# A two-layer graph network on one core: look-ups and gathers moved around the branch, and the last batch stored in natural order

## The chip, the cores and the metric

The kernel runs on one core of a Trainium2 chip. The metric is the device time of one execution in microseconds (us); a single core runs, so it is also the slowest. Five engines work side by side, each through its own queue of instructions and in its order: PE (TensorE, matmuls), DVE (VectorE), ACT (ScalarE), POOL (GpSimd) and SP (SyncE). Plain DMAs are issued by SP and ACT, and those with a list of row numbers (gathers and scatters) by POOL. An engine waits for another engine or for a DMA through semaphores.

## The reference

x is 32 batches of 512 rows of 512 floats, adj one 512 x 512 matrix, mostly zero, with weights between 0.05 and 1 on the diagonal and on some other entries. Two layers, each with a layer norm and a ReLU ahead of it:

```python
h = jnp.maximum(_layernorm(x, axis=-1), 0.0)
x = x + (jnp.einsum('nm,bmd->bnd', adj, h) @ weight + bias)       # layer 0
h = jnp.maximum(_layernorm(x, axis=-1), 0.0)
q, k, v = h @ Wq + bq, h @ Wk + bk, h @ Wv + bv                   # 8 heads
scores = q k^T / sqrt(64) + (1.0 - adj) * -1000000000.0
x = x + softmax(scores) v @ Wo + bo                               # layer 1
```

The mask is so strong that a row's softmax comes down to the column with the greatest adj, where that is certain. Layer 1 is then, for each row, one row of h (its source, `idx`) times the product Wv Wo, plus a constant row `cvo`.

## The kernel before, in words

A prologue (not touched) multiplies Wv and Wo, finds `idx`, and tests on the device whether each row has one clear source and few enough rows are sources. `single_path` is the path for that case.

**The loop.** `run_phase` goes through loops b = 0 to 32. Loop b holds, in this order on PE, layer 0 of batch b (seven products in the manner of Strassen, `product`, L534, whose results DVE adds onto x at L590), the aggregation adj @ h of batch b+1, and layer 1 of batch b-1 (seven products, results taken by DVE at L580 and ACT at L582). A batch's x lies in one of five tiles (`xs`).

**The order.** Each loop has 21 steps, one for each product or other piece of PE work. `put(batch, step, f)` hangs a piece of work of the other engines on a step, and the engines' queues get the work in that order, which no scheduler changes. POOL's indirect DMAs are also held back in time: `behind` makes each wait for the last result that an engine took from PE's accumulators before it in this order (`tick`), so that it goes out "in step".

**The plan.** Most entries of adj are zero. `Plan` (L1027) finds, in loops 0 to 3 and beside the dense work, an order of the rows in which adj becomes mostly empty. `xi` is the list of x rows in the new order for every batch, `gi` that of some extra rows. `schedule` hangs the plan's work on (loop, step) pairs. What the change touches: `tables` gathers the four row tiles of the reordered adj (`ap<-atd`, L1292), `tables_g` the three of the extra rows (`ag`), and `look_1` looks up, for each of the four tiles of `idx`, the new position of a row (`pi<-posd`, L1292), a gather of 128 numbers, after `posd` is written in loop 2. In loop 6 DVE casts `pi` at L1307 (`whole_pi`), PE turns the result over at L1297, and from this the second look-up `pq` (`look_2`) and the lists `place` and `home` are made.

**The branch.** Loops 0 to 3 run dense and in natural order. Ahead of loop FIRST = 4 every engine loads a flag and branches (L980 to L982). If the plan fits, loops 4 to 32 run with the sparse aggregation `spread` (L651, L654, L657): it multiplies h by the tiles of `ap`, one row tile after the other, and the normalised extra rows (`plan.HG`, in the tile `adjT`) by `ag`. From then on x of a batch is gathered in the new order by POOL (`load_x`, L506; in the profile under its helper's line, L497), the extra rows too (`load_g`, L666, `at<-in_x_dram,gi`), and the finished batches are scattered back to natural rows of the output by POOL (`store_rows`, L518). The extra rows of batches 5 and 6 are normalised by `lead` (statistics on ACT at L396, offset on DVE at L407, the ReLU on ACT at L381); later ones together with x.

**Layer 1 and its DRAM tables.** The h rows that are sources are written to a compact DRAM table `hs` (`put_h`; from a natural-order batch a POOL scatter for each of the four tiles, L694) and read back in another arrangement into `hc` (`get_h`, four SP DMAs, L705, each waiting for all four scatters), which DVE transposes to `hT` (L756). The products' result z is transposed by DVE (L770) and written to DRAM (`put_z`, L775), and POOL's gather `x<-z` adds each row's z to x (`finish`).

**The end.** For batches 29 and 30 (`back`), x is turned back to natural order: POOL scatters it into a DRAM tile (`turn_back`, L470), SP reads it back (`come_back`, L480), and the stores to the output are plain ones by SP or ACT (L512). Batch 31 stays in the new order. Its layer 1 is `layer1_rows`: POOL gathers, for all rows, the source rows of h (`get_all`, by `plan.pq`), PE transposes them (L717, copied by ACT at L718) and multiplies them row tile by row tile (r = 0 to 3, L729), DVE adds the result (L732), and the tile is scattered to the output by POOL (L518). After r = 0 DVE adds z of batch 29, and POOL starts to fetch z of batch 30 (`fetch`); after r = 2 and r = 3 DVE adds it, three tiles and one (L789).

Lines that the text names belong to the kernel before.

## Time and profile before

| What | Value |
|---|---|
| times of three runs | 1012.4, 1013.54, 1016.65 us; median 1013.54 |
| the profiled execution's own time | 1015.4 us |
| its span, from the first to the last instruction | 1013.7 us |
| mean granted clock of PE | 0.995 |
| busy: PE, DVE, POOL, ACT | 988.4, 801.1, 590.0, 585.3 us |
| moved by DMA | 208.89 MB, 206 GB/s over the span |
| branch passed by PE | 177.54 us |
| loops 4, 5, 6, 7, 8 | 28.93, 31.93, 31.54, 28.82, 28.82 us |
| PE begins the row tiles of the last batch | 985.63 us |
| last landing of a store | 1008.79 us |

All times count from the start of the span. The page gives sums over the whole span; queries of the trace give the same for a stretch, the waits of one engine with what ended them, and each engine's timeline. In a timeline a row is: start, length, engine, line, operation, output<-input, how many of them in a row, and in brackets the idle time ahead with what ended it ("issue" is time in which nothing that the profile shows was waited for). Issue and landing times of DMAs come from the trace's records of them.

### The profile page before, as it was taken

What the parts mean: (1) busy time and instruction counts of PE and PEld (TensorE: products, weight loads), DVE (VectorE), ACT (ScalarE), POOL (GpSimd) and SP (SyncE); (2) the same over time, 40 slices, a digit from 0 to 9 for tenths busy, and PEclk for the clock granted to TensorE, in tenths of its full rate; (3) what the DMA queues carried; (4) which work ended last, traced back from release to release, by engine and by line L of the source; (5) the groups of instructions that cost most, each with busy time, mean ns of one, the idle gap of its engine ahead of it and who ended that gap; (6) DMA issues with size and microseconds to landing.
All of it is one profiled execution on the core that took longest, in us unless ns stands there. A gap on an engine that the chain in (4) does not pass through costs nothing.

```text
span 1013.7 us, 17267 instructions
## 1 busy us (share of the span) xinstructions
PE 988.4 (98%) x5627; PEld 886.6 (87%) x5627; DVE 801.1 (79%) x1792; ACT 585.3 (58%) x1282; POOL 590.0 (58%) x667
## 2 busy tenths in 40 slices
PE   9999998999999999999999999999999999999985
PEld 7478887988899999999999999999999999999882
DVE  6998887767888777778887777778887777788773
ACT  4756444556665555566755555667655556676230
POOL 1033267656666666666666666666666666666543
PEclk9999999999999999999999999999999999999998
DMA  9214578889898888888888888888878888888867
GB/s 337 100 56 141 101 221 235 207 206 233 194 231 203 199 214 209 221 228 221 208 202 202 208 215 213 229 220 215 206 195 207 220 206 230 221 216 210 214 201 248
DMA packets 161883, 208.89 MB, mean 206 GB/s; under 512 B 16556, under 2 KB 104376, under 8 KB 161784
## 3 DMA queue, kind: packets, MB, share of 16 engines
q0 software_dynamic: 44544, 120.10, 48.4%
q1 hardware_dynamic: 115480, 85.66, 29.5%
q10 hardware_dynamic: 1760, 1.93, 0.6%
q8 instruction: 46, 0.75, 0.3%
q14 instruction: 53, 0.43, 0.2%
HBM read 123.55 MB, written 84.09 MB: 205 GB/s over the span
## 4 chain that ended last, share of the span: by engine, by line
PE 84%; DVE 7%; issue 3%; DMA 3%; ACT 1%; POOL 1%; SPq 0%; POOLq 0%; DVEq 0%; ACTq 0%
PE mm L534 59%; PE mm L654 13%; PE mm L657 7%; PE mm L651 2%; PE mm L675 1%; DVE st L363 1%; DMA hc<-hs 1%; DMA ap<-in_adj_dram,xi 1%; PE mm L273 1%; DVE x L590 1%; DVE x L629 0%; DMA hs<-h,dest 0%; PE pt L171 0%; DMA x<-xn 0%; ACT h L381 0%
## 5 line engine op out<-in xcount | busy, mean ns | idle before, releaser
L590 DVE TENSOR_TENSOR x<-mm,x 128x512 f32<-128x512 f32 x217 | 148.4, 686 | 135.9 <-PE mm L534 100.4
L497 POOL DMA_INDIRECT x<-z,pplace x96 | 153.4, 1598 | 81.5 <-ACT yT L662 40.9
L381 ACT ACTIVATE h<-x,off,rstd 128x512 f32<-128x512 f32 x256 | 196.1, 804 | 6.9 <-DVE off L372 3.6
L534 PE MATMUL mm<-w_t,sel 128*128 128x256 f32 x744 | 171.9, 380 | 3.1 <-DVE x L590 2.8
L367 ACT ACTIVATE rstd<-mv,eps 128x2 f32<-128x2 f32 (+1 forms) x90 | 26.3, 292 | 241.1 <-DVE mv L364 226.0
L534 PEld LDWEIGHTS mm<-w_t,sel 128*128 128x128 f32 x744 | 140.5, 190 | 23.6 <-DVE x L590 4.2
L363 DVE BATCH_NORM_STATS2 st<-x 128x6 f32<-128x512 f32 x234 | 157.5, 673 | 1.1
L654 PE MATMUL mm<-ap,h 128*128 128x256 f32 x648 | 157.8, 380 | 0.0
L518 POOL DMA_INDIRECT out_dram<-x,xi x100 | 124.6, 1246 | 45.7 <-DVE zs L580 19.8
L497 POOL DMA_INDIRECT x<-in_x_dram,xi x108 | 103.8, 961 | 72.0 <-issue 29.5
L654 PEld LDWEIGHTS mm<-ap,h 128*128 128x128 f32 x648 | 114.9, 191 | 11.1
L497 POOL DMA_INDIRECT at<-in_x_dram,gi x81 | 77.2, 953 | 72.0 <-DVE st L363 22.3
L534 PE MATMUL mm<-w_s,yT 128*128 128x256 f32 x496 | 117.3, 379 | 0.8 <-PE mm L534 0.8
L534 PE MATMUL mm<-hTs,wvo_t 128*128 128x168 f32 x720 | 113.6, 307 | 2.1 <-ACT zs L582 2.1
L534 PEld LDWEIGHTS mm<-hTs,wvo_t 128*128 128x128 f32 x720 | 105.4, 190 | 3.1 <-ACT zs L582 3.1
L582 ACT ACTIVATE zs<-mm,cvo_c 128x168 f32<-128x168 f32 x240 | 82.8, 397 | 41.4 <-PE mm L534 29.0
L534 PEld LDWEIGHTS mm<-w_s,yT 128*128 128x128 f32 x496 | 92.8, 190 | 12.3 <-issue 1.0
L657 PEld LDWEIGHTS mm<-ag,adjT 128*128 128x128 f32 x648 | 89.3, 191 | 5.6
L657 PE MATMUL mm<-ag,adjT 128*128 128x128 f32 x648 | 89.7, 275 | 0.0
L629 DVE TENSOR_TENSOR x<-x,b_r 128x512 f32<-128x512 f32 x124 | 83.9, 678 | 0.0
L662 ACT COPY yT<-mm 128x512 f32<-128x512 f32 x108 | 61.5, 570 | 31.5 <-PE mm L657 29.4
L534 PE MATMUL mm<-hT,wvo 128*128 128x168 f32 x480 | 78.3, 306 | 0.0
(324 smaller groups left out, 1677.3 us busy)
## 6 DMA issues: line engine op xcount, KB each, us to landing
hc<-hs SPq DMA_DIRECT2D x124, 176.0 KB
z<-zr SPq DMA_DIRECT2D x120, 96.0 KB
hs<-h SPq DMA_DIRECT2D x52, 192.0 KB
z<-zr SPq DMA_DIRECT2D x120, 80.0 KB
hs<-h SPq DMA_DIRECT2D x52, 160.0 KB
out_dram<-x SPq DMA_DIRECT2D x26, 256.0 KB
x<-in_x_dram SPq DMA_DIRECT2D x12, 256.0 KB
x<-xn SPq DMA_DIRECT2D x8, 256.0 KB
```

The lines of the kernel that those rows point to most:

```text
L363: self.nc.vector.bn_stats(st, self.src[:, self.chunks[i], :])
L367: self.nc.scalar.activation(self.rstd[:, 0:len(self.chunks)], self.mv[:, :, 1], AF.Sqrt, bias=self.eps)
L381: self.nc.scalar.activation(dst, src, AF.Relu, bias=self.off[:, i:i + 1], scale=self.rstd[:, i:i + 1])
L497: return behind(nc.gpsimd.indirect_dma_start(out=dst, out_offset=None, in_=rows, in_offset=bass.IndirectOffsetOnAxis(ap=at, axis=0), **more))
L518: stored = behind(nc.gpsimd.indirect_dma_start(out=out_rows, out_offset=bass.IndirectOffsetOnAxis(ap=plan.xi[:, b, c:c + 1], axis=0), in_= ...
L534: nc.tensor.matmul(bank[:, m, 0:half], lhs[:, k, m * P:(m + 1) * P], rhs[:, k, :], start=(first and m == 0 and k == 0), stop=(k == 1), ski ...
L582: taken = nc.scalar.activation(dst[:, m, :], bank[:, m, :], AF.Identity, bias=cvo_c[:, 2 * i + m:2 * i + m + 1])
L590: return nc.vector.tensor_add(dst, bank, dst)
L629: nc.vector.tensor_add(X[b][:, c, :], X[b][:, c, :], b0_r)
L654: nc.tensor.matmul(two(bank, j), H0[b][:, j, cols], two(plan.ap[:, j, :], j), start=False, stop=False, skip_group_check=True)
L657: nc.tensor.matmul(bank[:, j * P:(j + 1) * P], extra[:, j - 1, cols], plan.ag[:, j - 1, j * P:(j + 1) * P], start=False, stop=(j == C - 1) ...
L662: tick(nc.scalar.copy(yT[:, d, :], bank))
```

## The change

PE's instructions keep their order. What changes is where the other engines' work stands:

- **Look-ups.** `look_1` moves from loop 5 (steps 14, 16, 17, 18) to loop 2 (steps 14 and 15) and loop 3 (steps 8 and 9). On POOL the first two then stand between the third and the fourth scatter of `hs`, ahead of the gathers of adj rows (`ap<-in_adj_dram`) and of x of batch 5; the other two stand between `x<-z` of batch 1 and the scatters of `hs` of batch 3.
- **Tables.** The row tiles 2 and 3 of `ap` are gathered in loop 4, steps 3 and 4, behind the branch and behind the three gathers of `ag`, and no longer at the end of loop 3.
- **Gathered tiles.** The extra rows of batch 6 are gathered in loop 5, steps 0 to 2 (loop 4, steps 15, 17, 19 before); those of batch 7 in loop 5 at steps 7, 8, 10 (6, 7, 8 before). `lead` works on batch 6 two steps later; all of its activations come at step 6.
- **x of two batches later.** `load_x` of batch 6 moves to steps 5 to 8 of loop 4 (3 to 6 before), that of batch 7 to steps 3 to 6 of loop 5 (0 to 3 before).
- **The end.** Batch 31 is turned back too (`turn_back` at steps 7 to 10 of loop 31, `come_back` at step 15), its source rows are gathered by `plan.pi`, and its stores become plain SP stores. Batch 30 is turned back in loop 30 and read back at its step 18, and no longer in loops 31 and 32. `come_back` is two DMAs of 512 KB in place of four of 256 KB. The z of batches 29 and 30 is sent in four DMAs, not eight. `finish` of batch 28 comes at steps 4 to 7 of loop 30. The fetch of z of batch 30 no longer stands behind the store of r = 0, and its adds follow r = 1 (one tile) and r = 2 (three).

```diff
@@ -463,7 +463,7 @@
         def back(b):
-            return sparse and ordered and B - 3 <= b < B - 1
+            return sparse and ordered and B - 3 <= b
 
@@ -476,8 +476,9 @@
         def come_back(b):
-            for c in range(C):
-                load = nc.sync.dma_start(X[b][:, c, :], xn_d[b % 3][c * P:(c + 1) * P, :])
+            rows = xn_d[b % 3].rearrange("(c p) d -> p c d", p=P)
+            for c in (0, 2):
+                load = nc.sync.dma_start(X[b][:, c:c + 2, :], rows[:, c:c + 2, :])
                 for stored in PUT[-b]:
@@ -623,7 +624,7 @@
             H0[b] = hs[b % 2]
-            return norm(X[b], H0[b], range(C), kind)
+            return norm(xs[b % 5], H0[b], range(C), kind)
 
@@ -709,7 +710,7 @@
             for c in chunks:
-                gather(hs[0][:, c, :], hs_d[b % 3], idx[:, c, 0:1] if natural(b) else plan.pq[:, c:c + 1])
+                gather(hs[0][:, c, :], hs_d[b % 3], idx[:, c, 0:1] if natural(b) else plan.pi[:, c:c + 1])
 
@@ -734,9 +735,8 @@
                         add_z(B - 3, c, nc.sync)
-                    fetch(B - 2)
-                if sparse and r >= 2:
-                    for c in ((0, 1, 2), (3,))[r - 2]:
+                if sparse and 0 < r < C - 1:
+                    for c in ((0,), (1, 2, 3))[r - 1]:
                         add_z(B - 2, c, nc.scalar if c % 2 else nc.sync)
@@ -764,15 +764,23 @@
 
-        def put_z(b, s0, s1, quarters=range(4)):
-            zr = hc_t if b == B - 2 else zr_t
-            if 0 in quarters:
-                nc.vector.transpose(zr[:, s0:s1, :].rearrange("p s (c e) -> p s c e", c=4),
-                                    zt(b)[:, :, 32 * s0:32 * s1].rearrange("p c (s j) -> p s c j", j=32))
+        def zr(b):
+            return hc_t if b == B - 2 else zr_t
+
+        def turn_z(b, s0, s1):
+            nc.vector.transpose(zr(b)[:, s0:s1, :].rearrange("p s (c e) -> p s c e", c=4),
+                                zt(b)[:, :, 32 * s0:32 * s1].rearrange("p c (s j) -> p s c j", j=32))
+
+        def send_z(b, s0, s1, quarters=range(4)):
             rows = z_d[b % 3].rearrange("(s j) (q f) -> q j s f", j=32, q=4)
...
                 eng = nc.scalar if q > 1 and b == B - 2 else nc.sync
-                eng.dma_start(rows[q][:, s0:s1, :], zr[32 * q:32 * q + 32, s0:s1, :])
+                eng.dma_start(rows[q][:, s0:s1, :], zr(b)[32 * q:32 * q + 32, s0:s1, :])
+
+        def put_z(b, s0, s1):
+            turn_z(b, s0, s1)
+            send_z(b, s0, s1)
+
 
@@ -814,14 +822,18 @@
             if sparse and b <= FIRST + 1:
+                late = 2 * (b - FIRST)
                 for j in range(3):
-                    put(b + 1, 1 + j, lambda b, j: lead.stats(j), j)
-                put(b + 1, 3, lambda b: lead.power())
-                put(b + 1, 5, lambda b: lead.offset())
+                    put(b + 1, 1 + late + j, lambda b, j: lead.stats(j), j)
+                put(b + 1, 3 + late, lambda b: lead.power())
+                put(b + 1, 5 + late // 2, lambda b: lead.offset())
                 for j in range(3):
-                    put(b + 1, 5 + (j + 1) // 2, lambda b, j: lead.relu(j), j)
+                    put(b + 1, 6 if late else 5 + (j + 1) // 2, lambda b, j: lead.relu(j), j)
             if sparse:
-                for j, step in enumerate((15, 17, 19) if b == FIRST else (6, 7, 8) if b == FIRST + 1 else (4, 5, 6)):
+                if b == FIRST + 1:
+                    for j in range(3):
+                        put(b + 1, j, load_g, [j])
+                for j, step in enumerate(() if b == FIRST else (7, 8, 10) if b == FIRST + 1 else (4, 5, 6)):
                     put(b + 2, step, load_g, [j])
@@ -831,14 +843,15 @@
                 for c in range(C):
-                    put(b + 2, c + 3 if sparse and b == FIRST else c, load_x, [c])
+                    put(b + 2, c + (5 if b == FIRST else 3 if b == FIRST + 1 else 0), load_x, [c])
             elif folded and not ordered and b == FIRST:
...
             elif b < B:
-                for c, step in enumerate((9, 11, 13, 15) if sparse and b == FIRST + 1 else (7, 9, 11, 13) if sparse else
+                for c, step in enumerate((9, 11, 13, 15) if sparse and b == FIRST + 1 else (4, 5, 6, 7) if sparse and b == B - 2 else
+                                         (7, 9, 11, 13) if sparse else
                                          (4, 5, 6, 7) if ordered and b == FIRST - 1 else (1, 2, 3, 4)):
@@ -853,10 +866,16 @@
                     put(b + 1, step, h0_sum, i)
-            late = sparse and b > B - 1
-            put(b - 2, 14 if b == B - 1 else 0, put_z, 0, 6, range(2 if late else 4))
-            if b == B - 1:
-                put(b - 2, 13, put_z, 6, S)
+            if sparse and b >= B - 1:
+                if b == B - 1:
+                    put(b - 2, 13, turn_z, 6, S)
+                    put(b - 1, 20, turn_z, 6, S)
+                put(b - 2, 14 if b == B - 1 else 0, turn_z, 0, 6)
+                put(b - 2, 14 if b == B - 1 else 0, send_z, 0, S, range(4 if b == B - 1 else 2))
+            else:
+                put(b - 2, 14 if b == B - 1 else 0, put_z, 0, 6)
+                if b == B - 1:
+                    put(b - 2, 13, put_z, 6, S)
             for r, step in enumerate((10, 11, 12) if b in (1, B - 1) else (5, 7, 8) if b < B else ()):
@@ -899,18 +918,23 @@
                     put(b, 13, get_all, [c])
-                    put(b - 1, 2 * c, turn_back, [c])
+                    put(b, 7 + c, turn_back, [c])
+                if sparse:
+                    put(b, 15, come_back)
             if sparse and b == B - 2:
...
                     put(b - 1, c, turn_back, [c])
+                    put(b, (8, 10, 11, 12)[c], turn_back, [c])
                 put(b - 1, 9, come_back)
+                put(b, 18, come_back)
             for i, step in enumerate((12, 13, 13, 14) if b in (1, B - 1) else (11, 11, 12, 12) if b < B else ()):
...
             if b < B and b != B - 2:
-                put(b - 1, 20, put_z, 6, S, range(2 if sparse and b == B - 1 else 4))
+                if not (sparse and b == B - 1):
+                    put(b - 1, 20, put_z, 6, S)
             ahead = []
@@ -943,11 +967,10 @@
                 put(b - 1, 1, lambda b: transpose_all(0))
-                put(b - 2, 2, put_z, 6, S, range(2, 4))
-                put(b - 2, 2, put_z, 0, 6, range(2, 4))
-                put(b - 2, 2, come_back)
+                put(b - 2, 2, send_z, 0, S, range(2, 4))
                 for c in range(C):
                     put(b - 1, 1, add_cvo, c)
+                put(b - 2, 3, fetch)
             if b == 1:
@@ -1390,11 +1413,13 @@
         at(3, 8, self.save_at, 2)
-        move(3, (11, 13, 19, 20), self.tables)
+        move(3, (11, 13), self.tables)
+        move(4, (3, 4), lambda behind, c: self.tables(behind, c + 2))
         move(4, (0, 1, 2), self.tables_g)
...
             at(4, 4 + j, self.mask_g, j)
-        move(5, (14, 16, 17, 18), self.look_1)
+        move(2, (14, 15), self.look_1)
+        move(3, (8, 9), lambda behind, c: self.look_1(behind, c + 2))
         at(6, 2, self.whole_pi)
```

## The prediction

> **What bounds the kernel now.** I read the page first: one engine fills the span, and the chain that ended last runs through it.
>
> ```profile
> PE 988.4 (98%) x5627; PEld 886.6 (87%) x5627; DVE 801.1 (79%) x1792; ACT 585.3 (58%) x1282; POOL 590.0 (58%) x667
> ...
> PE 84%; DVE 7%; issue 3%; DMA 3%; ACT 1%; POOL 1%; SPq 0%; POOLq 0%; DVEq 0%; ACTq 0%
> ```
>
> The change leaves TensorE's instructions as they are, in number and order. It can win only where TensorE waits, and lose only where it makes TensorE wait or lengthens the tail. So the second view is busy time loop by loop (stretch, its length, then busy time and instructions of each engine, clock, DMA share): loops 3, 4, 5, 6, an undisturbed loop (8), and the end from the last product of layer 1 on.
>
> ```profile
> 139.07:177.54 38.47, 34.83 (x186) 30.74 (x184) 28.16 (x57) 14.45 (x30) 24.98 (x27) 1.00 0.88 246
> 177.54:206.47 28.93, 28.93 (x169) 26.86 (x170) 23.20 (x52) 14.72 (x33) 19.62 (x21) 1.00 0.82 209
> 206.47:238.40 31.93, 29.82 (x171) 26.71 (x169) 22.97 (x52) 22.22 (x52) 18.48 (x18) 1.00 0.82 196
> 238.40:269.94 31.54, 29.62 (x171) 26.76 (x170) 23.30 (x53) 17.67 (x39) 19.59 (x19) 1.00 0.87 223
> 298.76:327.58 28.82, 28.82 (x170) 26.71 (x169) 24.72 (x60) 17.88 (x39) 18.44 (x19) 1.00 0.85 220
> 985.63:1013.70 28.07, 17.01 (x44) 7.96 (x44) 10.37 (x17) 1.76 (x3) 10.97 (x15) 0.83 0.74 246
> ```
>
> Loop 5 is 31.93 − 28.82 = 3.1 us too long and loop 6 is 2.7; loop 4 is not. That 5.8 us is nearly all there is to win around the branch. The waits of TensorE (total, times, longest) say where:
>
> ```profile
> PE mm L534 <- DVE x L590: 2.8, 3, 1.8
> PE mm L729 <- ACT h0s L582: 2.6, 1, 2.6
> PE mm L534 <- ACT zs L582: 2.1, 3, 1.4
> ...
> PE pt L1327 <- DMA ap<-in_adj_dram,xi: 0.6, 1, 0.6
> ```
>
> The 1.8 falls at 215.31 (loop 5), the 1.4 at 264.14 (loop 6). VectorE's timeline (start, length, group, idle before) names what made it late in the two loops, and GpSimd's shows the queue behind that:
>
> ```profile
> 220.30 0.71 DVE L756 STREAM_TRANSPOSE hT<-hc 128x512 f32<-128x512 f32 x1 [1.98 <-DMA hc<-hs]
> 245.46 0.21 DVE L1307 CAST pqf<-pi 128x4 f32<-128x4 int32 x1 [2.72 <-DMA pi<-posd,idx]
> ```
>
> ```profile
> 135.46 1.42 POOL L694 DMA_INDIRECT hs<-h,dest  x1 [0.19 <-DVE gi L1289]
> 137.19 1.02 POOL L1292 DMA_INDIRECT ap<-in_adj_dram,xi  x1 [0.19 <-ACT h L381]
> 141.43 0.95 POOL L1292 DMA_INDIRECT ap<-in_adj_dram,xi  x1 [0.30 <-issue]
> 205.72 0.98 POOL L694 DMA_INDIRECT hs<-h,dest  x1 [0.30 <-issue]
> 209.53 0.95 POOL L497 DMA_INDIRECT x<-in_x_dram,xi  x1 [0.30 <-issue]
> 1003.64 1.16 POOL L518 DMA_INDIRECT out_dram<-x,xi  x1 [1.70 <-DVE x L732]
> ```
>
> In loop 8 the same L756 starts 9.45 us after the loop does (308.21); in loop 5 it starts after 13.8. In loop 6 the CAST of the looked-up positions stands in VectorE's queue ahead of the takes.
>
> **Part 1: look-ups into loops 2 and 3 (a gain in loop 6, a price in loop 2).** The four pi gathers leave GpSimd's loop 5 (issued 233.22 to 240.13, last landing 245.44). In loop 6 the 2.72 us wait goes, and with it what follows from it: TensorE's 0.26 + 0.28 around 246 and the 1.38 at 264.14, 1.9 us of waits, out of 2.7 over a plain loop. The loop keeps its transpose and casts. I take −2.2 (bounds −2.7 and −1.0, the last if only the short waits and half of the long one go).
>
> Two of the four now stand in loop 2 between the third and the fourth scatter of hs. One pi gather holds GpSimd for 0.95 to 1.50 us, median 1.07, plus 0.30 to the next. From 135.46 to 146.86 GpSimd goes from one DMA straight to the next, so 2 x (0.95 + 0.30) = 2.5 us push the fourth scatter, the four adjacency gathers, four x gathers, and, on SyncE, the reads of hc that wait for the scatters, with the z stores queued behind them. The last adjacency gather, issued at 141.43, landed at 148.78, and TensorE's L1327 already waited 0.64 for it: no cover is left. Issued at 143.93 instead, it would take 6.50 by the row of the x gather issued then: landing 150.4, 1.6 us later; with 7.36 as now, 2.5. I take **+2.0**. Ends: +2.9 with the dearer gathers, +0.4 if the bytes, not the issue, set the landing. The other two, in loop 3, push hs, the at gathers and the reads of hc by 2.5. Those reads landed at 180.40 and are wanted by L756 at 187.47; the two tables taken out of the end of loop 3 give GpSimd the same 2.5 back. Cost 0; if that cover is gone, up to 2.5.
>
> **Part 2: tables c2 and c3 behind the branch.** They take the places at which x of batch 6 was gathered (183.99 and 185.72; landings 189.0 and 189.6). The sparse products start at 189.73 and reach row tile 3 near 190.6. About 1 us to spare: cost 0, but by the slowest row near, 8.86 us for a gather at 212.04, it would land at 194.6, +4.0. Behind them x of batch 6 comes two steps later; its last tile is issued near 194.9 and lands near 199 where VectorE's statistics asked for it at 198.76: 0, at most +1.
>
> **Part 3: extra rows (load_g) and x of loops 4 and 5.** Without a g gather between the last two scatters of hs, but with two gathers more ahead of them, the fourth scatter comes out at about 206 against 205.72: no gain in itself. What changes is what flies beside the reads of hc. Before, those reads, issued 210.31 to 211.69, took 5.33 to 8.53 us beside the x gathers of batch 7, issued from 209.53 on. After, each x gather is tied to an eviction three steps later (near 213.6, 215.3, 217.0), so the reads share the DMA with two or three g gathers only. The same reads at 174.04 to 175.42 took 3.66 to 4.98. So hc lands near 216 and not at 220.22, and L756 stands at its usual 9.5 us. Of the 3.1 I take **−2.3**; ends −3.1 and +0.3 (all four scatters 0.5 late and the reads as slow as before). The 1.78 at 215.31 is not clear to me: VectorE had been idle 3.75 us for a piece that TensorE seemed to have ended, so some of the 3.1 may stay. What is late next: the extra rows of batch 6. Their last gather goes at about 210.8 and lands near 215; two ScalarE passes, offset and three 0.8 us activations end near 219.6, and L657 wants the first at 222.12 less the gain, 219.8. Tight, priced 0 to +1.
>
> **Part 4: the end.** The last landing is GpSimd's store of the last tile: issued 1003.64, landed 1008.79, 5.14 us. After, SyncE issues it once L732 ends (1002.68 + 0.69), about 1003.4. SyncE's and ScalarE's stores of 256 KB there took 3.75 to 4.18 us, so it lands at 1007.2 to 1007.6: **−1.3**, ends −2.1 (2.96, the fastest) and 0. The late z fetches move ahead by about 4 us, and the adds of batch 30 fit into the 3.2 us that VectorE idles between L732s; the L729 chain bounds, and nothing is won there. GpSimd idles 10.59 us ahead of the h gathers (977.66); turn_back(31), four scatters of 0.96 + 0.3, fits in. come_back(31) brings 1 MB more on SyncE at about 977 to 981. Behind it wait two z stores only; beside it fly the h gathers, whose first landed at 982.06 for a transpose at 982.43. Cost 0, ends −2.0 and +2.0: the first L732 comes 5.9 us after L729 starts, the next 3.9 apart; the granted clock was 0.50 from 986.83 to 990.24 after the 2.60 us wait. A shorter wait might save those 2.0; late gathers could add as much.
>
> [...]
>
> **Sum.** +2.0 − 2.3 − 2.2 − 1.3 = −3.8 on the profiled execution's 1015.4 (span 1013.7 and 1.7 around it): 1011.6. The median of the runs shown is 1013.54, 1.86 below that execution; the same −3.8 from it gives **1009.7**. About 0.5% (5.07 us) is what a measurement can tell from no change: faster means below 1008.47, slower above 1018.61.
>
> **Rivals.** (B) The price in loop 2 is hidden, or the clock in the tail does not drop: −3.8 − 2.0 = −5.8, both −7.8; 1005.7 to 1007.7. For it: landings of 6 to 7 us say that the DMA is crowded. Against: from 130 to 138 it is nearly idle, so issue counts. (C) hc still lands at 220, since the z stores, also issued from 213 on, share the DMA: −1.5, 1012.0. (D) Slower: the table's last tile after the branch. If it lands 4 us after row tile 3 is reached, +4.0, and everything GpSimd issues behind it, hs and then hc, is that much later, so loop 5 gains nothing: −3.8 + 4.0 + 2.3 = +2.5, 1016.0. It decides from a landing past 194.4, where the 3.8 is eaten. Against: the two x gathers at that place took 5.0 and 3.9 us. (E) The change doesn't do what it says: with pi gone, loop 6 waits as long for the next thing (its x gathers waited 3.66 for the out stores): −1.6, 1011.9.
>
> **How the numbers follow.** Forecast 0.46, B 0.22, C 0.17, D 0.09, E 0.06. The forecast's own spread, 1007.5 to 1011.5, has 0.10 below 1008.47, B nearly all: faster 0.31. Half of D with a late end on top passes 1018.61: slower 0.04. Same 0.65. The range reaches into B and to D's edge: 1005.2 to 1015.0.
>
> **What would show it.** Right: no CAST wait in loop 6 and its length near 29.3; L756 of loop 5 within 10 us of the loop's start; L1327 waiting 2 to 3 us near 149; last landing about 5 us ahead of the span's end, by SyncE. Wrong: L1327's wait unchanged (B), a wait of L654 on ap near 191 (D), L717 or L729 waiting for h gathers past 984, or L657 for adjT in loop 5.

## The result, and the profile after

The changed kernel is slower: **1023.14 us** median (1020.19 to 1027.64, 7 runs) beside 1016.65 of the kernel before, run on the same chip (1012.4 to 1018.59, 7 runs). The ratio of runs taken in turn is 1.0078, 95% interval 1.0057 to 1.0098, so about +7.9 us where −3.8 was forecast (the two medians lie 6.5 apart). 1009.7 was the prediction, 1005.2 to 1015.0 its range. The profiled execution of after took 1027.64 us and is the slowest of its seven; its span is 11.9 us longer than that of before. So its stages are read below for what happens, and the ratios for what it is worth.

The page of after, first the sums, then the clock in 40 slices:

```profile
span 1025.6 us, 17256 instructions
...
PE 993.8 (97%) x5627; PEld 891.0 (87%) x5627; DVE 801.8 (78%) x1792; ACT 586.0 (57%) x1282; POOL 590.6 (58%) x667
...
PEclk9999999998999999999999999999999999999998
```

TensorE runs as many instructions as before, 5627, but is busy 5.4 us longer (993.8 against 988.4): some of them ran on a slower clock (granted 0.988 in the mean, against 0.995). The rest of the loss is in its waits (total, times, longest):

```profile
PE mm L658 <- ACT adjT L381: 5.0, 1, 5.0
PE mm L535 <- DVE zs L581: 4.1, 2, 3.1
PE pt L1350 <- DMA ap<-in_adj_dram,xi: 2.9, 3, 1.7
PE mm L535 <- ACT zs L583: 1.9, 3, 0.8
...
PE mm L535 <- DVE x L591: 1.0, 2, 0.5
PE pt L718 <- DMA h<-hs,pi: 1.0, 1, 1.0
```

(Lines below the edits moved: L535, L591, L658, L706, L1315 and L1350 of after are L534, L590, L657, L705, L1292 and L1327 of before; L756, L381, L403, L406 and L407 kept their numbers.) The two waits of before that Part 1 and Part 3 were to remove, 1.8 on L590 and 1.4 on zs, are gone or shorter. In their place stand a wait for `adjT` that before did not have, and waits for `ap` that sum to 2.93 us against 0.64. (The 3.1 on zs L581 belongs to a pause at the branch, see the last section; before has 1.76 there.) From the start of one loop's layer-0 product to the next, loops 3 to 6 took 45.39, 30.60, 37.03 and 29.82 us (before 38.47, 28.93, 31.93, 31.54); all later loops are 28.82 in both, and the end, from layer 0 of batch 31 on, is 60.35 against 60.17.

**The first place, the start of loop 3.** GpSimd's timeline shows the two look-ups ahead of the last scatter and the gathers of `ap`; TensorE's shows what waits for them:

```profile
135.21 1.44 POOL L1315 DMA_INDIRECT pi<-posd,idx  x1 [0.19 <-DVE gi L1312]
136.96 0.98 POOL L1315 DMA_INDIRECT pi<-posd,idx  x1 [0.30 <-ACT h L381]
138.25 1.00 POOL L695 DMA_INDIRECT hs<-h,dest  x1 [0.30 <-issue]
...
143.71 0.95 POOL L1315 DMA_INDIRECT ap<-in_adj_dram,xi  x1 [0.30 <-issue]
```

```profile
148.17 0.33 PE L1350 MATMUL pt<-ident,ap 128*128 128x128 f32 x1 [0.44 <-DMA ap<-in_adj_dram,xi]
150.24 0.48 PE L1350 MATMUL pt<-ident,ap 128*128 128x128 f32 x1 [1.74 <-DMA ap<-in_adj_dram,xi]
151.47 0.47 PE L1350 MATMUL pt<-ident,ap 128*128 128x128 f32 x1 [0.75 <-DMA ap<-in_adj_dram,xi]
```

The last gather goes at 143.71, 2.3 us later than before (141.43), and the waits sum to 2.93 against 0.64: +2.3, where the prediction took +2.0. That much was right. What it left out stands in the next view (stretch, length, busy time and count of PE, PEld, DVE, ACT, POOL, then the granted clock, DMA share and GB/s):

```profile
146.60:150.10 3.50, 1.46 (x7) 0.84 (x5) 0.71 (x2) 0.00 (x0) 2.84 (x3) 1.00 1.10 279
150.10:156.90 6.80, 5.91 (x17) 4.61 (x18) 2.15 (x4) 1.17 (x2) 0.84 (x1) 0.50 0.60 219
156.90:163.70 6.80, 6.80 (x37) 6.01 (x36) 5.34 (x15) 2.84 (x7) 5.58 (x5) 1.00 0.88 175
```

From 150.1 on, still within the waits, the granted clock is 0.50 for 6.8 us, in which TensorE gets through 17 matmuls where the next 6.8 us hold 37. Matched matmul by matmul, after is 2.6 us later behind the waits and 5.3 behind the slow stretch.

**The second place, loop 5.** VectorE first, ScalarE and TensorE then:

```profile
231.11 0.71 DVE L756 STREAM_TRANSPOSE hT<-hc 128x512 f32<-128x512 f32 x1 [6.77 <-DMA z<-zr]
231.74 0.65 DVE L591 TENSOR_TENSOR x<-mm,x 128x512 f32<-128x512 f32 x1
232.32 0.15 DVE L406 RECIPROCAL rstd<-rstd 128x3 f32<-128x3 f32 x1
232.51 0.16 DVE L407 TENSOR_TENSOR off<-sum,rstd 128x3 f32<-128x3 f32 x1
```

```profile
227.07 0.30 ACT L403 ACTIVATE rstd<-sq,eps 128x3 f32<-128x3 f32 x1
232.71 2.22 ACT L381 ACTIVATE adjT<-at,off,rstd 128x512 f32<-128x512 f32 x3 [5.34 <-DVE off L407]
```

```profile
233.57 2.21 PE L658 MATMUL mm<-ag,adjT 128*128 128x128 f32 x6 [4.99 <-ACT adjT L381]
```

ScalarE has `rstd` at 227.4. The two small instructions that make the offset from it take 0.3 us, but they now stand behind L756 in VectorE's order, and L756 waits for `hc`, whose last read landed at 231.03 (the profile puts the end of this wait down to `z<-zr`, another DMA). In before they stood ahead of L756, which started at 220.30:

```profile
217.95 0.17 DVE L406 RECIPROCAL rstd<-rstd 128x3 f32<-128x3 f32 x1
218.15 0.16 DVE L407 TENSOR_TENSOR off<-sum,rstd 128x3 f32<-128x3 f32 x1
```

So three activations, 2.22 us in all, that TensorE needs wait on a transpose with which they have nothing to do; TensorE idles 4.99 us, and the clock is again 0.50, from 232.01 for 6.83 us. Nor did `hc` come sooner: L756 starts 16.3 us into loop 5, against 13.8 before and the 9.5 that was forecast. Its four reads were issued 6.5 to 7.9 us into the loop (3.8 to 5.2 in before), and the last took 8.31 us (8.53).

### The profile page after: what moved, and what is told of

Its sections match the earlier page's. It is cut to its first block, busy times and chain, and to the rows that moved or that the text cites. A ratio compares the mean times of both kernels' runs of the same rounds, so it can differ in the third digit from the quotient of the medians.

```text
span 1025.6 us, 17256 instructions
## 1 busy us (share of the span) xinstructions
PE 993.8 (97%) x5627; PEld 891.0 (87%) x5627; DVE 801.8 (78%) x1792; ACT 586.0 (57%) x1282; POOL 590.6 (58%) x667
## 5 line engine op out<-in xcount | busy, mean ns | idle before, releaser
L591 DVE TENSOR_TENSOR x<-mm,x 128x512 f32<-128x512 f32 x217 | 148.8, 686 | 139.6 <-PE mm L535 107.4
L381 ACT ACTIVATE h<-x,off,rstd 128x512 f32<-128x512 f32 x256 | 195.9, 804 | 6.8 <-DVE off L372 3.6
L535 PE MATMUL mm<-w_t,sel 128*128 128x256 f32 x744 | 171.6, 380 | 1.0 <-DVE x L591 1.0
L535 PEld LDWEIGHTS mm<-w_t,sel 128*128 128x128 f32 x744 | 140.8, 190 | 21.2 <-DVE x L591 2.0
L519 POOL DMA_INDIRECT out_dram<-x,xi x96 | 120.4, 1254 | 38.6 <-DVE zs L581 19.4
L535 PE MATMUL mm<-w_s,yT 128*128 128x256 f32 x496 | 119.0, 383 | 0.8 <-ACT zs L583 0.8
L535 PE MATMUL mm<-hTs,wvo_t 128*128 128x168 f32 x720 | 113.4, 307 | 1.1 <-ACT zs L583 1.1
L535 PEld LDWEIGHTS mm<-hTs,wvo_t 128*128 128x128 f32 x720 | 105.4, 190 | 1.7 <-ACT zs L583 1.6
L535 PEld LDWEIGHTS mm<-w_s,yT 128*128 128x128 f32 x496 | 93.8, 192 | 12.7 <-ACT zs L583 1.0
L658 PEld LDWEIGHTS mm<-ag,adjT 128*128 128x128 f32 x648 | 90.3, 193 | 11.5 <-ACT adjT L381 5.8
L658 PE MATMUL mm<-ag,adjT 128*128 128x128 f32 x648 | 91.2, 277 | 5.0 <-ACT adjT L381 5.0
L535 PE MATMUL mm<-hT,wvo 128*128 128x168 f32 x480 | 78.3, 306 | 0.0
```

What stands on the lines that cost most here:

```text
L381: self.nc.scalar.activation(dst, src, AF.Relu, bias=self.off[:, i:i + 1], scale=self.rstd[:, i:i + 1])
L519: stored = behind(nc.gpsimd.indirect_dma_start(out=out_rows, out_offset=bass.IndirectOffsetOnAxis(ap=plan.xi[:, b, c:c + 1], axis=0), in_= ...
L535: nc.tensor.matmul(bank[:, m, 0:half], lhs[:, k, m * P:(m + 1) * P], rhs[:, k, :], start=(first and m == 0 and k == 0), stop=(k == 1), ski ...
L591: return nc.vector.tensor_add(dst, bank, dst)
L658: nc.tensor.matmul(bank[:, j * P:(j + 1) * P], extra[:, j - 1, cols], plan.ag[:, j - 1, j * P:(j + 1) * P], start=False, stop=(j == C - 1) ...
```

## The experiments

Each table value is a ratio to the kernel before, run in turn with it on the same chip. They come from four series (four, four, four and three rows of the table). The median of before was 1017.59 us in the first, 1011.12 in the second, 1015.23 in the third and 1010.27 in the fourth; what is known of this difference stands at the end.

| kernel | ratio | 95% interval |
|---|---|---|
| 1: the change, offset at its old step | 1.0053 | 1.0035 to 1.0071 |
| 2: the change, look-ups back in loop 5 | 1.0012 | 0.9990 to 1.0033 |
| 3: the end alone (Part 4) | 1.0020 | 1.0002 to 1.0038 |
| 4: the branch alone (Parts 1 to 3) | 1.0065 | 1.0044 to 1.0086 |
| 5: the change, offset and look-ups both back | 1.0006 | 0.9997 to 1.0016 |
| 6: before, look-ups at the start of loop 3 | **0.9978** | 0.9965 to 0.9991 |
| 7: look-ups alone (Part 1) | 1.0036 | 1.0023 to 1.0049 |
| 8: before, x of batch 7 three steps later | **0.9973** | 0.9963 to 0.9983 |
| 14: the end without batch 31's turn | 1.0000 | 0.9984 to 1.0015 |
| 12: before, look-ups as above and x later | 0.9988 | 0.9971 to 1.0005 |
| 9: extra rows and x alone (Part 3) | 1.0024 | 1.0006 to 1.0042 |
| 11: tables alone (Part 2) | 1.0015 | 0.9999 to 1.0031 |
| 10: Part 3 with the offset at its old step | 1.0018 | 1.0005 to 1.0031 |
| 13: the change with three places mended | **0.9984** | 0.9970 to 0.9998 |
| 15: the end, 31's turn without its transfers | 0.9988 | 0.9977 to 0.9999 |

**1. The change, offset at its old step.**

```
-                put(b + 1, 5 + late // 2, lambda b: lead.offset())
+                put(b + 1, 5, lambda b: lead.offset())
```

> The changed kernel with one step number undone: the offset of the extra rows of batch 6 is hung on step 5 again and not on step 6, which puts it ahead of the transpose of hc (L756) in VectorE's queue; everything else stays as changed. Theory A (the queue behind L756): TensorE's 4.99 us wait for adjT in loop 5 falls below 1 us, the half clock that followed it (232.01 to 238.84) does not come, and loop 5 shortens from 37.0 us to about 30; the kernel stands within 2 us of the kernel before. Rival B (hc itself): L756 still starts 16 us into loop 5, and TensorE waits as long for the takes that stand behind it; the kernel stays 5 us or more slower than before.

The wait for `adjT` fell to three of 0.42, 0.22 and 0.22 us, as expected of the place, and loop 5 to 32.23 us, where about 30 was expected. The kernel did not come within 2 us of before, as theory A had it: it stays 5.4 us slower, which is rival B's number, though L756 starts 13.8 us into loop 5 and not 16. The two ratios differ by 1.0078 − 1.0053, 2.5 us, and their intervals overlap. Most of the loss stays, so the offset is not the main cost.

**2. The change, look-ups back in loop 5.**

```
-        move(2, (14, 15), self.look_1)
-        move(3, (8, 9), lambda behind, c: self.look_1(behind, c + 2))
+        move(5, (14, 16, 17, 18), self.look_1)
```

> The changed kernel with the four look-ups back in loop 5 (steps 14, 16, 17, 18); everything else stays as changed. Theory A (the look-ups in loop 2 push the adjacency gathers, and the wait costs twice, once as a wait and once as half clock behind it): the three waits of the adjacency transposes, 2.93 us in all, fall to about 0.6, the half clock from 150.09 to 156.92 does not come, loop 3 shortens by 4 to 5 us, and loop 6 gets back 1 to 2.7 us; net 2 to 4 us faster than the changed kernel. Rival B (the wait of 3.11 us and the half clock at the branch make loop 3 long, whatever stands in loop 2): loop 3 shortens by 2.3 at most, and the kernel is not faster than the changed one.

6.7 us of the 7.9 are gone, more than the 2 to 4 expected. In its profile one `ap` wait of 0.77 remains, and the mean granted clock is 0.996 against 0.988 in after; that execution is the fastest of twelve (1014.65, median 1019.39). The look-ups' place is the largest single cost. The offset is still late here, yet the longest wait for `adjT` is 1.7.

**3 and 4. The end alone, the branch alone** (the hunks of the diff on either side, put into the kernel before).

> The kernel before with the changed end alone: batch 31 turned back, its stores by SyncE, z of batches 29 and 30 sent in four DMAs, batch 30 turned back in loop 30, the fetch of z of batch 30 freed. Nothing around the branch changes. The prediction's step: 1.3 us faster than before, through the last store. Theory A (what the trace of the changed kernel suggests): the 1 MB that comes back on SyncE and the four scatters slow the h gathers from 3.2 to 4.4 us to 5.8 to 6.9 and the z fetches to 7.7, which eats the gain: within 1 us of the kernel before. Rival: slower by 2 us, since the last additions wait for the z fetches.

> The kernel before with the changes around the branch alone (look-ups, tables, extra rows, x of two batches later); the end is that of the kernel before. Theory A (all of the loss stands around the branch): slower than before by what the whole change costs, 6 to 7 us, with the 5 us wait for adjT in loop 5 and about 3 us of waits for the adjacency rows in loop 3. Rival: a part of the loss comes from the end, and this kernel is at most 4 us slower.

1.0020 and 1.0065 make 1.0085 together, against 1.0078 for the whole. The end costs about 2 us instead of saving 1.3, as the rival of experiment 3 had it. In 4 the longest wait for `adjT` is 1.9 and not 5.

**5. Offset and look-ups both back in the change.**

> The changed kernel with the look-ups back in loop 5 and the offset of batch 6's extra rows back at step 5, both at once; new end, tables behind the branch, extra rows and x moved as in the change. Theory A (the look-ups in loops 2 and 3 and the late offset are the branch's cost; the new end costs about 2 us): 1017 to 1019 us beside 1017 of before, loop 3 near 39.5, loop 5 near 31.5, no wait of TensorE over 1 us for a gather of `ap` and none for `adjT`. Rival B (moving x and the extra rows costs by itself too): 1020 or more, and loop 5 stays above 32 us with another wait in it.

1.0006, as theory A had it: what is left of the change, taken together, can't be told from nothing. Loop 3 is 35.64 us, loop 5 31.74; the longest `adjT` wait was 0.8.

**6. The look-ups where GpSimd was idle.**

```
-        move(5, (14, 16, 17, 18), self.look_1)
+        move(3, (0, 1, 2, 3), self.look_1)
```

> The kernel before, with only its four look-ups of `pi` moved, from loop 5 to steps 0 to 3 of loop 3, where GpSimd's queue is free behind the gathers of `ap`. Theory A (what costs is that the look-ups stand ahead of the gathers of `ap`, and loop 5 without look-ups is worth little): 1016 to 1018, within 0.1% of before; no wait for `ap`, loop 6 stays at 31 or above. Rival, the prediction's Part 1 (taking them out of loop 5 is worth 2.2 us in loop 6): 1014.5 to 1015.5, loop 6 under 30. Rival B (look-ups cost wherever they stand in loops 2 and 3): 1020 or more.

The rival won: 0.9978, 2.2 us faster than before, the sum that Part 1 had for loop 6. Loop 6 is 28.93 us, against 29.8 to 31.5 in the four profiles whose work around the branch is that of before (before itself and experiments 3, 14 and 15); loop 5 gives a part back, 32.46 against 31.3 to 31.9. GpSimd's queue shows the look-ups (here the first of four) between the x gathers, behind the last gather of `ap`; they take up the stretch in which it had idled 5.79 us:

```profile
141.27 0.95 POOL L1292 DMA_INDIRECT ap<-in_adj_dram,xi  x1 [0.30 <-DVE zr L770]
142.52 0.95 POOL L497 DMA_INDIRECT x<-in_x_dram,xi  x1 [0.30 <-issue]
143.77 0.94 POOL L1292 DMA_INDIRECT pi<-posd,idx  x1 [0.30 <-issue]
145.02 1.38 POOL L497 DMA_INDIRECT x<-in_x_dram,xi  x1 [0.30 <-DVE x L590]
```

**7. The look-ups alone, where the change has them.**

> The kernel before, with only its four look-ups moved to where the change has them (two in loop 2 at steps 14 and 15, two in loop 3 at steps 8 and 9). Theory A (they push the gathers of `ap` back, and TensorE waits for those and then runs at half clock): about +5, 1021 to 1023; waits for `ap` of 2 us and more in sum at the start of loop 3, a stretch of half clock just behind, loop 3 over 43 us. Rival (the wait is as in A, but is made good by loop 6, as the prediction's Part 1 summed it: +2.3 and -2.2): 1016.5 to 1018.5.

1.0036, +3.6 us, less than the +5 of theory A, more than the 0 of its rival. Against experiment 6, which differs in the look-ups' place alone, the loops tell both halves: loop 6 is 28.93 in both, and loop 3 is 39.95 against 36.01. Of these 3.9, 2.1 are waits (2.03 and 0.75 against 0.70; first line of the waits experiment 7, second 6), and the rest is the clock:

```profile
PE pt L1327 <- DMA ap<-in_adj_dram,xi: 2.8, 2, 2.0
PE pt L1327 <- DMA ap<-in_adj_dram,xi: 0.7, 1, 0.7
```

```profile
148.40:151.80 3.40, 1.41 (x7) 1.12 (x8) 0.71 (x1) 0.59 (x1) 0.94 (x1) 1.00 1.08 386
151.80:155.20 3.40, 3.40 (x12) 2.76 (x11) 1.51 (x4) 0.59 (x1) 0.00 (x0) 0.51 0.48 172
```

Half of 3.4 is 1.7: 2.1 + 1.7 = 3.8 of the 3.9. By the medians the two kernels lie 5.5 us apart. The profiled execution of experiment 7 is 1.7 below its median and had a mean clock of 0.994, the median of its twelve executions one of 0.992 (before in this series 0.995), which points to more half clock in the others.

**8. x of batch 7 later.**

```
-                    put(b + 2, c + 3 if sparse and b == FIRST else c, load_x, [c])
+                    put(b + 2, c + (3 if b in (FIRST, FIRST + 1) else 0), load_x, [c])
```

> The kernel before, with only the gathers of x of batch 7 moved from steps 0 to 3 of loop 5 to steps 3 to 6. The prediction's Part 3 (they run beside the reads of h of batch 4, which so land late): the reads land 2 to 4 us sooner, the transposes at L756 start nearer to 10 us into loop 5 than to 13.8, and loop 5 and 6 are 1.5 to 2.3 us shorter in sum, 1014.5 to 1016. Rival (the reads are late because the last row scatter of batch 4 is issued late, and x gathers take little from them): transposes still at 12.5 us or later, time within 0.5 us of before.

0.9973: 2.7 us faster, by one line (and the buffer name that goes with it). The last of the four reads of `hc` took 5.58 us from issue to landing, against 8.53 in before, where x flies beside them. L756 starts 11.8 us into loop 5, against 13.8 in before and 14.4 in experiment 6; the offset still stands ahead of it:

```profile
214.93 0.16 DVE L407 TENSOR_TENSOR off<-sum,rstd 128x3 f32<-128x3 f32 x1
217.05 0.71 DVE L756 STREAM_TRANSPOSE hT<-hc 128x512 f32<-128x512 f32 x1 [1.96 <-DMA hc<-hs]
```

Loops 5 and 6 take 29.86 and 30.16. This is Part 3's mechanism, and about its price, though L756 does not come at the forecast 9.5. (In the four profiles with the branch of before the last read took 7.0 to 8.5 us; in experiment 12, which has this edit too, L756 starts at 11.3.)

**9. Extra rows and x as the change has them, nothing else.**

> The kernel before with the prediction's Part 3 alone, whole, as the change has it: extra rows of batch 6 and their normalization later, x of batches 6 and 7 later; look-ups, tables and end as before. The prediction's Part 3: -2.3 us, 0.9975 to 0.998. Theory A (x alone gives 0.9973, and the offset at step 6, behind the transposes that wait for h of batch 4, gives it back): a wait of TensorE of 1.5 us or more for `adjT` in loop 5, ratio 0.999 to 1.003.

1.0024, a loss of 2.4 us; theory A held. ScalarE's L403 for `rstd` of the extra rows starts 13.5 us into loop 5 (8.3 in before, 9.1 in experiment 8), L756 starts at 15.4, the offset comes behind it at 16.8, and TensorE waits:

```profile
225.99 2.21 PE L657 MATMUL mm<-ag,adjT 128*128 128x128 f32 x6 [4.05 <-ACT adjT L381]
```

**10. The same with the offset at its old step.**

> The kernel before with the prediction's Part 3, but the offset of batch 6's extra rows at step 5 as before instead of step 6. Theory A (of Part 3 only the offset's place costs, about 5 us; x alone gives 0.9973): no wait of TensorE for `adjT` over 0.8 us in loop 5, ratio 0.997 to 0.999. Rival (the later rows and x crowd GpSimd's queue in loop 5 by themselves): waits of 1 us or more remain in loops 5 and 6, ratio 1.000 to 1.002.

Here theory A failed: no wait for `adjT` over 0.22 us, loop 5 at 31.92 instead of 36.59, and still 1.0018. The ratios make the offset worth 0.6 us here, 0.6 between experiments 2 and 5, and 2.5 in experiment 1, each time with overlapping intervals. In the four profiles with the late offset (after and experiments 2, 4 and 9) the longest wait for `adjT` is 4.99, 1.7, 1.9 and 4.05 us, and L756 starts 16.3, 13.0, 13.2 and 15.4 us into loop 5: the later `hc`, the longer the wait. So the wait is seen, and it is long only where `hc` is late; its price in the ratios is not told from nothing. What remains is that x's gain is gone: L756 starts 13.8 us into the loop, as in before. The rows' gathers stand between the last scatters and x on GpSimd: the last scatter goes 0.5 us into loop 5 (in before 0.8 before it), the third row gather at 4.6, and the reads of `hc`, issued at 4.9 to 6.4, take 5.9 to 7.4. Where x alone was moved, the last row gather went 2.3 us into the loop. So, by the order of the queue, the rows took x's place beside the reads. A lost gain makes 1.000; where the 1.8 us above it come from is not shown.

**11. Tables alone.**

> The kernel before with the prediction's Part 2 alone: the tables of columns 2 and 3 built in loop 4, behind the branch. The prediction: 0, at the end of its range +4 us. Theory A (their gathers push the scatter of h of batch 4 and with it the reads in loop 5 by about 1 us): loop 5 longer by 0.5 to 1.5, loop 3 no shorter, ratio 1.000 to 1.0015. Rival (the two gathers taken from ahead of the branch let it start earlier): 0.998 to 0.999, loop 3 shorter by 1 to 2 us.

1.0015, and the interval includes 1. Its profile has a pause of 1.7 at the branch that other kernels have too (below), and loop 5 at 31.64 is no longer than in before. A cost of Part 2 is not shown.

**12 and 13. Both gains together; the change mended.** The second is the changed kernel with the look-ups as in 6, the offset as in 1 and batch 31 not turned back.

> The kernel before with the two edits that gained alone: look-ups at steps 0 to 3 of loop 3 (0.9978) and x of batch 7 three steps later (0.9973). Theory A (they save different time: the look-ups loop 6, x loop 5): loop 5 near 30, loop 6 near 29, together 1.1 to 1.5 us below either, ratio 0.9955 to 0.9965. Rival (both save the same idle time of TensorE behind the late reads of h of batch 4): 0.997 to 0.998.

> The changed kernel with three places mended: look-ups at steps 0 to 3 of loop 3, the offset at step 5, batch 31 not turned back. Tables behind the branch, extra rows and x later and the rest of the end stay. Theory A (nothing else of the change costs): ratio 0.997 to 0.9995, no wait for `ap` or `adjT` over 0.9 us. Rival (tables and extra rows cost too, by what they put on GpSimd's queue): 1.000 to 1.002.

The two gains don't add: 0.9988, and its interval takes in either alone. Loops 5 and 6 sum to 59.6 us, against 60.0 with x alone, 61.4 with the look-ups alone and 61.4 to 63.5 in the four profiles with the branch of before: most of it is the same idle time, and the 0.4 left can't be told in a series with pauses of 1.7 to 3.9 at the branch. The mended change, at 0.9984, is faster than before, so no harm of the rest of it is seen; nor is x's gain, since the look-ups alone give 0.9978. Experiments 6 and 8 gain as much with a line or two each.

**14 and 15. The end without batch 31's turn; without its transfers only.** In 14, batch 31 is treated as before. In 15 only its four scatters and two reads are left out, so that h is added to x rows of another order: that kernel serves for its time alone.

```
-                    put(b, 7 + c, turn_back, [c])
-                if sparse:
-                    put(b, 15, come_back)
```

> The kernel before, with the end of the change but without its turning back of batch 31: batch 31 keeps its own order (look-ups of `pq`, stored through GpSimd as before), while batches 29 and 30 are turned back, sent and fetched as in the change. Theory A (the cost of the new end, 1.0020 as a ratio, is batch 31's turn: four more scatters and two more reads beside the gathers of h): 0.999 to 1.000. Rival (it is the earlier turn of batch 30 and the later fetch of batch 30's z): 1.0015 to 1.003, as the whole end.

> The kernel before with the whole new end, but without the transfers of batch 31's turn: its four scatters and two reads are left out, so that its x rows stay in their old order while h is looked up and stored in natural order. Theory A (the end's loss is those transfers, which run beside the gathers of h, the put of z and its fetch): ratio 0.9985 to 1.000, z of batch 30 lands in under 5.5 us against 8.4 with them. Rival (it is the new order itself, the store on SyncE's queue behind VectorE's add): 1.0015 to 1.0025.

1.0000 and 0.9988 against 1.0020 with everything. So the new end without those transfers is 1.2 us faster than before (interval 0.1 to 2.3), near the 1.3 of the prediction's store, and with them 2.0 slower: by two series, they cost 3.2. That the 1.2 is the store's alone is not shown, as the intervals of 14 and 15 overlap. The profiles agree: from the first product of loop 30 on, the five kernels with the whole new end (after, 1, 2, 3, 5) took 79.6 to 81.2 us, 14 and 13 took 79.2 and 78.6, and 15 took 77.4; the nine with the end of before took 78.6 to 82.1.

The chain that ended last shows where: with the transfers (experiment 3, first fence) the put of batch 30's z takes 8.38 us to land, without them (15, second fence) 5.11, and its fetch can only begin behind it. The put is also issued later, since ScalarE, which issues half of it, does so behind its copy of the first transposed h rows, and their gather is late (6.27 in the first line). The fetch of z starts 61.0 to 62.7 us into this stretch in the five kernels with the transfers, and 57.2 to 57.9 in the three without.

```profile
982.11 6.27 DMA h<-hs,pi
989.87 8.38 DMA z<-hc
998.32 0.70 issue
1000.48 6.46 DMA yT<-z,phome
```

```profile
979.59 5.11 DMA z<-hc
...
989.22 7.34 DMA yT<-z,phome
```

On VectorE, the adds of batch 30's z (L797) stand between the L733 that take TensorE's results, and wait for that fetch. In after:

```profile
DVE x L797 <- DMA yT<-z,phome: 6.3, 2, 3.9
```

## Why the prediction was wrong

| part | predicted, us | alone, us (ratio − 1, times before) |
|---|---|---|
| 1, look-ups | +2.0 − 2.2 | +3.6 |
| 2, tables | 0 | +1.5, not told from 0 |
| 3, extra rows and x | −2.3 | +2.4 |
| 4, the end | −1.3 | +2.0 |
| whole | −3.8 | +7.9 |

- **Part 1.** Right: the wait for `ap` (+2.3 for +2.0), and the gain of taking the look-ups out of loop 5 (experiment 6: −2.2 for −2.2). Wrong: the step that priced the wait at its own length, up to "+2.9 with the dearer gathers". It cost 3.9 of loop 3 in experiment 7, since a stretch at half clock goes with it (3.4 us at 0.51). The prediction had such a stretch before its eyes at 986.83, behind a wait of 2.60, and put it into the end alone; Part 1 made a wait of the same size and took no clock for it. In the profiles that makes +3.9 − 2.2 = +1.7 of the +3.6 measured; the other half is not located, save for the lower clock of the other executions. (Against rival B it also read the DMA as "nearly idle" from 130 to 138: its share there is 0.35, and only from 132 to 135 is it near nothing.)
- **Part 2.** 0 is within what was measured; rival D, the table's tile after the branch, did not come: TensorE's longest wait for it was 0.64 us (experiment 11).
- **Part 3.** The step "hc lands near 216 and not at 220.22" failed. What it rested on, that x beside the reads makes them slow, is shown by experiment 8 (5.58 us for the last read without x, 8.53 with it in before). But it counted the two gathers put ahead of the scatters as "no gain in itself", with the last scatter about 0.3 us later, and the row gathers behind them as "two or three g gathers only". In after and in experiment 10 the last scatter is 1.1 and 1.2 us later in the loop than in before, and the reads take 5.9 to 7.4 us beside the row gathers in experiment 10. This much of rival C came true: `hc` was no sooner. And the step for what is late next, "two ScalarE passes, offset and three 0.8 us activations end near 219.6 … Tight, priced 0 to +1", read the offset's time from its inputs and not from VectorE's queue. One step later put it behind an instruction that waits for a DMA: 4.99 us in after, and half clock behind it. The prediction itself named "L657 for adjT in loop 5" among the signs of being wrong.
- **Part 4.** The store's gain is borne out as far as it can be told (1.2 for 1.3, the new end without 31's transfers). Wrong was "Cost 0" for the transfers of batch 31's turn: the prediction checked that there is a free place in the issuing queues, saw the h gathers beside them, and put "late gathers" at the far end of its range, +2.0. It did not follow them on to the put of batch 30's z and its fetch, which 2 MB more in flight make late (8.38 us for the put in experiment 3, 5.11 in 15); they cost 3.2. So the step that "the adds of batch 30 fit into the 3.2 us that VectorE idles between L732s" failed too: in after they wait for the fetch, 3.88 and 2.44 us, ahead of L733.
- **Rivals.** None described the whole. D came to the right side by a cost at the table's tile that did not come, and at +2.5.

The sum of the parts alone, 9.5, is 1.6 more than the whole; with intervals of 1.3 to 2.1 us on each that is no discrepancy. Experiment 5 shows one: tables, extra rows and x with the offset at its old step, and the new end cost 1.5 + 1.8 + 2.0 = 5.3 us one by one, and 0.6 (−0.3 to 1.6) together. The parts were measured in series whose `before` differ by up to 7.3 us. So the size of each of these three is open; what stands firm is the cost of the look-ups' place, 3.6 + 2.2 = 5.8 us between experiments 7 and 6, within one series.

## What to carry to other kernels

Moving an instruction on an in-order engine is priced by what then stands ahead of it: one step later meant here behind a wait for a DMA, and 4.99 us of TensorE. A wait of TensorE of some 2 us is to be priced with the stretch at half clock that may follow, which in experiment 7 cost about as much again (1.7 us beside 2.1). And a queue with room for an issue says nothing about the landings beside it (the put of z took 8.38 us with the transfers beside it, 5.11 without): three moves (x later, look-ups in an idle stretch, the store on SyncE with the transfers for it left out) each gained on its own, the last by 1.2 us, barely clear of noise. In the change, x's gain went where row gathers came beside the same reads, the look-ups' where they stood ahead of gathers that TensorE waits for, and the store's by the transfers that it needs.

## What the runs showed of the hardware

**When the clock dropped.** In after, stretches at half clock start at 150.09, 184.22 and 232.01, which is 10 and 14 steps of 3.413 us apart, and last two, one and two of these steps (6.83, 3.41 and 6.83 us). So thirteen profiles (before, after and experiments 1 to 5, 7, 9 to 12 and 14) were read in windows of that length around the branch and in the end, some 138 to 258 us and 960 to 996 us of each: every one of these windows is at 1.00 or at 0.50 as a whole. Take the busy share of TensorE in them. Each of the fifteen windows at full clock with 0.43 or less was followed by half clock, of those at 0.44 to 0.46 two out of five, and of those at 0.48 to 0.75 none. In after, 1.38 of 3.41 us (0.40) was too little; in before, 1.64 of 3.42 (0.48) was enough (PE's busy time is the first number behind the comma, the granted clock the third from the end):

```profile
146.68:150.09 3.41, 1.38 (x7) 0.77 (x5) 0.69 (x1) 0.00 (x0) 2.77 (x3) 1.00 1.09 279
150.09:153.50 3.41, 2.51 (x7) 1.86 (x8) 0.71 (x1) 0.59 (x1) 0.00 (x0) 0.50 1.04 381
```

```profile
212.00:215.42 3.42, 1.64 (x9) 1.11 (x8) 0.85 (x2) 3.35 (x9) 0.95 (x1) 1.00 1.01 195
215.42:218.83 3.41, 3.41 (x16) 3.02 (x17) 1.37 (x4) 0.85 (x2) 0.94 (x1) 1.00 1.12 208
```

A window that was itself at half clock was followed by another in the five cases in which it was busy for 0.86 or less, and not in those at 0.88 or more. So in these profiles half clock goes less with a single long wait than with some 1.9 us of idling within one window (0.56 of 3.41): in after it was the 0.44 and 1.59 of the 1.74, the rest of which falls into the next window.

**A pause at the branch that differs from run to run.** Around the end of loop 3, where each engine reads the flag and branches, TensorE paused for 0.78 us ahead of its next product in every profile of the second and fourth series, and for 1.7 to 4.2 us, there or within three products ahead, in all eight of the first and third. One of the longest, from experiment 14, with the releaser that the profile found:

```profile
178.77 3.78 PE L535 MATMUL mm<-w_s,yT 128*128 128x256 f32 x8 [3.87 <-remote]
```

With the half clock behind it (in experiment 14 0.50 from 176.60 to 183.43), such a pause is about the size of the difference between the series: before took 1011.12 and 1010.27 in the second and fourth, 1017.59 and 1015.23 in the first and third, with a median clock of 0.995 and 0.996 against 0.993 and 0.994. It comes with each kernel, so it is not of the change; two series on one chip differ in it, so it is not the chip either. What sets it stays open: in this execution the products ahead of it ended at 174.90, and the chain that ended last puts the next 3.11 us down to "another core or an unknown queue", though a single core runs. The wait on zs L581 of 3.1 in after stands at the same place; I count it as that pause, which no experiment could take away.
